# First-layer scores from exact high and low parts in one-pass products, keys one attention ahead, and a result whose heads stay in SBUF

## The chip, the core and the metric

The program runs on one core of a Trainium2 chip. The metric is device time in microseconds. The kernel before took 924.34 us (median of 3 runs, 924.27 to 926.34). Its profile comes from one more execution, which took 923.17 us; the span that the profile shows of it is 921.2 us.

The engines appear by short names: PE (TensorE, matrix products; PEld is its loading of weights), DVE (VectorE), ACT (ScalarE), POOL (GpSimd) and SP (SyncE, which here issues DMAs). SBUF is the memory on the chip that the engines compute from, PSUM the memory that products are written to, DRAM the large memory outside.

## The reference

16 sequences of 256 tokens with 256 features, and a context y of the same shape, go through three attentions of 16 heads (16 features a head) and one MLP:

```
layer 0: q = rms(x) Wq, k = rms(y) Wk, v = rms(y) Wv          (cross-attention, no positions)
         x = rms(x + softmax(q k^T / 4) v Wo)
layer 1: h = ln(x);  q, k, v from h; rotary positions on q, k;  causal;  x = x + a Wo
layer 2: h = ln(x);  q from h, k, v from y; rotary positions;   not causal;  x = x + a Wo
MLP:     x = x + gelu(ln(x) W1 + b1) W2                        (256 -> 1024 -> 256)
```

All of it is float32. The attention of a head is a product of 256 x 16 queries with 16 x 256 keys (the *scores*), an exponential, and a product of the result with the values; sums of the exponentials come from an extra column of the values, and the division is done on the result.

## The kernel before

**Attentions in one list.** The 48 attentions (3 layers x 16 sequences) stand in one hand-written order, `ORDER`, in which each digit is a layer: `000001010102210210210121021012210101021212122222`. Attention `i` is the i-th digit. The loop over `i` (with `n` for its blocks) writes out the order on every engine by hand: while attention `i` computes scores and values, the pieces for `i + 1` (query, key, value products), the end of `i - 1` and `i - 2` (heads, reciprocal, division, output product) and the statistics of `i + 2` are put between its blocks. Each engine runs its instructions strictly in that order; semaphores hold one back until its inputs are there. SP's queue of DMAs is in order too, so a DMA that waits holds up those behind it.

**Blocks.** An attention that isn't causal has 4 blocks: two tiles `t` of 8 heads, times two halves `kc` of the 256 keys. A causal one (layer 1) has 3. In block `n`, TensorE does the scores of block `n` (`scores`, line 569), then the values of the block before (`value`, line 609), then one dense product of 256 x 256 x 256 (`by_feature`, line 352, or `by_token`, line 364): the query, key or value of the next attention, or the output product of the last but one. In a causal attention the middle block has two dense products.

**Scores.** A tile of 128 partitions has 8 heads of 16 features, in four groups of 32 partitions with 2 heads each. A product contracts over a group of 32 and so over both heads. The query is therefore kept twice in `qm` (index `i` of 2), each copy with the other head's 16 partitions set to zero by a multiplication with `parity`. One product takes 64 keys and 2 x 256 queries (one column range for each copy); eight of them, on 4 row groups and 2 column groups of the array, make a block. ScalarE then takes the exponential of the four PSUM banks, in two instructions of 128 x 1024 (line 581). The tag `S` has two buffers, and a block uses both, so its scores wait for the exponentials of the block before.

**First layer's query and key.** `q` (line 487) writes both masked copies with two VectorE instructions from PSUM, times `rq`, the reciprocal norms of x spread over the partitions; `rq` is sent to DRAM and read back on all partitions (`send`, `receive`). `k` copies the key out of PSUM on ScalarE (line 527).

**The result's way.** The values' product leaves 32 partitions for each head (16 features, a sum, unused ones). `take` copies them to `av_sb` (line 626) and writes that to DRAM (line 627); `end` reads the sums (line 634) and the 16 features of each head (line 639) back, into a dense `oT`. `invert` takes reciprocals of the sums, sends them through DRAM to get them on all features of a head (lines 648, 654), and `divide` multiplies (line 660).

**The MLP** runs after the attentions on pairs of sequences, with 7 products for 8. Sums of its weights for that (`combine`, line 725) are made on GpSimd between the attentions.

Of the kernel before, what the change touches and what calls it, by code (L numbers as in the profile page):

```python
# [8 lines left out]
F32 = mybir.dt.float32  # L9
U8 = mybir.dt.uint8  # L10
I32 = mybir.dt.int32
AF = mybir.ActivationFunctionType
ALU = mybir.AluOpType
AX = mybir.AxisListType

P = 128
# [12 lines left out]
N_ATT = 3 * B  # L29

# [13 lines left out]
SWAP = [(i // HD) * HD + (i + HD // 2) % HD for i in range(32)]  # L44
# [29 lines left out]
def xattn_kernel(  # L74
# [45 lines left out]
    def batch(b):  # L120
# [3 lines left out]
        ys[b] = work.tile([P, NC, D], F32, tag="y", name=f"y{b}", bufs=3)  # L124
# [125 lines left out]
    def mean_squares(src, tag):  # L250
        ms = small.tile([P, NC], F32, tag=f"ms_{tag}", name=f"ms_{tag}")
        for c in range(NC):
            sq = work.tile([P, D], F32, tag="sq", name="sq", bufs=1)
            nc.vector.scalar_tensor_tensor(  # L254
                sq, src[:, c, :], 1.0 / D, src[:, c, :], ALU.mult, ALU.mult,
                accum_out=ms[:, c : c + 1],
            )
        return ms
# [112 lines left out]

    class Att:
        def __init__(self, i):
# [16 lines left out]
            self.pts = {}  # L390

# [17 lines left out]
        def spread(self):  # L409

            self.rq = work.tile([P, S], F32, tag="rq", name="rq")
# [21 lines left out]
        def receive(self):  # L433
            if self.layer == 0 and self.i > 1:
                self.rq = work.tile([P, S], F32, tag="rq", name="rq")
# [44 lines left out]

        def q(self, both=True):
            ps = by_feature(self.hT, self.w, 0)
            self.qm = work.tile([P, KC, 2, S], F32, tag="qm", name="qm", bufs=2)
# [14 lines left out]
        def second_mask(self):  # L498
            if self.layer > 0:
                nc.scalar.activation(  # L500
                    self.qm[:, :, 1, :], self.rotated_q, AF.Copy, scale=parity[1]
                )

        def first_qk(self):


            self.qm = work.tile([P, KC, 2, S], F32, tag="qm", name="qm", bufs=2)
            self.kT = work.tile([P, KC, S], F32, tag="kT", name="kT", bufs=2)
# [11 lines left out]
        def k(self):  # L520
            ps = by_feature(self.kvT, self.w, D)
            self.kT = work.tile([P, KC, S], F32, tag="kT", name="kT", bufs=2)
# [6 lines left out]
        def v(self):  # L529
            ps = by_token(self.kvT, self.w, 2 * D)  # L530
            va = self.va
            if self.layer == 0:
                m2 = slice(NC * self.b, NC * self.b + NC)
                nc.gpsimd.tensor_copy(
                    va[:, :, :, 16], mask01[:, m2].unsqueeze(2).to_broadcast([P, NC, H])
                )
                for c in range(NC):
                    nc.vector.tensor_scalar(
                        va[:, c, :, 0:HD], ps[:, c, :].rearrange("p (h d) -> p h d", d=HD),
# [3 lines left out]
            else:  # L543
                row = R_SAV if self.layer == 1 else R_CAV
                nc.gpsimd.memset(va[:, :, :, 16], 1.0)
                nc.vector.tensor_tensor(
                    va[:, :, :, 0:HD], ps.rearrange("p c (h d) -> p c h d", d=HD),
# [5 lines left out]
        def scores(self, n):  # L553
# [7 lines left out]
            pss = [psS.tile([P, 2, 512], F32, tag="S", name="S") for g in range(2)]  # L561
            for u, (t, _) in enumerate(units):
                for half in range(2):
                    keys = slice(64 * half, 64 * half + 64)
                    at = slice(kc * P + 64 * half, kc * P + 64 * half + 64)
                    for g, ps in enumerate(pss):
                        for j in range(2):
                            r = slice(32 * (2 * g + j), 32 * (2 * g + j) + 32)
                            nc.tensor.matmul(  # L569
                                ps[keys, j, 2 * m * u : 2 * m * (u + 1)]  # L570
                                .rearrange("p (i s) -> p i s", i=2),
                                lhsT=self.kT[r, t, at],
                                rhs=self.qm[r, t, :, q0:S],
                                start=True, stop=True, skip_group_check=True,
                            )
# [23 lines left out]
        def value(self, t, kc):  # L599
# [15 lines left out]
            if final and t == 0:  # L615
                self.av_sb = work.tile([P, KC, 2, S], F32, tag="av", name="av")
                self.sums = work.tile([P, 2, 2 * H], F32, tag="sums", name="sums")
                self.oT = work.tile([P, KC, S], F32, tag="oT", name="oT")

                self.hop = dram.tile([KC, 2, P, S], F32, tag="hop", name="hop")  # L620
                self.take(t, nc.scalar.copy)

        def take(self, t, copy):

            av = self.av_sb[:, t]
            copy(av, self.av)  # L626
            nc.sync.dma_start(out=self.hop[t].rearrange("i p q -> p i q"), in_=av)

        def end(self, copy=nc.vector.tensor_copy):


            self.take(1, copy)
            heads = self.hop.rearrange("t i (r e) q -> (t i r) e q", e=32)
            nc.sync.dma_start(
                out=self.sums[:, 0],
                in_=heads[:, HD, :].rearrange("g (a b) -> g a b", b=2 * H),
            )
            for t in range(KC):
                nc.sync.dma_start(out=self.oT[:, t], in_=heads[8 * t : 8 * t + 8, :HD])

        def invert(self, beside=lambda: None):

            sums = self.sums
            if self.layer == 0:
                nc.vector.tensor_scalar(sums[:, 0], sums[:, 0], 1e-30, None, ALU.max)
            nc.vector.reciprocal(sums[:, 1], sums[:, 0])
            hop = dram.tile([KC, 8, S], F32, tag="inv", name="inv_hop")
            nc.sync.dma_start(
                out=hop.rearrange("t g (a b) -> (t g a) b", b=2 * H), in_=sums[:, 1]
# [3 lines left out]
            for t in range(KC):  # L653
                nc.sync.dma_start(
                    out=self.inv[:, t], in_=hop[t].unsqueeze(1).to_broadcast([8, HD, S])
# [46 lines left out]
    up_s = [ctile([P, H1], f"up_s{n}") for n in (1, 2, 4)]  # L702
    down_t = [ctile([P, FF // P // 2, H2], f"down_t{n}") for n in (1, 2, 4)]
# [7 lines left out]
    def combine():  # L711

        s1, s2, s4 = up_s
        t1, t2, t4 = down_t
        for o, a, b, op in (
            (s1, up_a(1, 0), up_a(1, 1), ALU.add),
            (s2, s1, up_a(0, 0), ALU.subtract),
            (up_a(1, 0), up_a(0, 0), up_a(1, 0), ALU.subtract),
            (s4, up_a(0, 1), s2, ALU.subtract),
# [6 lines left out]
            yield  # L726

    class Mlp:
# [106 lines left out]
        def up(self, n):  # L835
# [6 lines left out]
            elif n == 5:  # L842
                self.Z = psS.tile([P, 2, 512], F32, tag="S", name="upZ")
                self.Z = [self.Z[:, i] for i in range(2)]
                self.up_product(5, self.Z, up_s[0], ts[0], True)
                self.keep_sum(1, 1, self.Z)
            elif n == 6:
                self.up_product(6, self.X, up_s[1], ts[1], False)
# [8 lines left out]
            elif n == 3:  # L857
                self.up_product(3, self.Z, up_s[2], b(1, 1), False)
# [793 lines left out]
```

## Time and profile before

| | |
|---|---|
| time, median of 3 runs | 924.34 us |
| the profiled execution, its span | 923.17 us, 921.2 us |
| TensorE busy | 908.0 us (99%) |
| VectorE busy | 684.6 us (74%) |
| ScalarE busy | 531.7 us (58%) |
| GpSimd busy | 346.5 us (38%) |
| scores (line 569) | 197.8 us busy, 3072 records |
| values (line 609) | 188.8 us busy, 3072 records |
| granted clock of TensorE | full, in all slices |
| bytes moved by DMA | 100.72 MB, 109 GB/s |

The attentions take up the span to about 735 us, the MLP the rest. A float32 product of the program shows as two records on TensorE. Records of products that run side by side overlap, so the busy time of a row, not count times mean, is what it takes.

### The profile page before, as it was taken

The numbers are of one execution on the slowest core, as the hardware profiler recorded it, in microseconds if no ns is written. First come the engines' busy times: TensorE is split into PE (matmuls) and PEld (weight loads), VectorE is DVE, ScalarE is ACT, GpSimd is POOL, SyncE is SP. The second block draws the span as 40 slices with busy tenths as digits, with TensorE's granted clock in tenths as the row PEclk, the third lists the DMA queues.
The fourth block names the chain that finished last, engine by engine and source line by source line (L and its number), as shares of the span: only waits on it lengthen the run. The fifth ranks groups of instructions, "written<-read, shape, count | busy, mean of one in ns | idle before, by whom it ended". The sixth has DMA issues, their size and how long they took to land.

```text
span 921.2 us, 32418 instructions
## 1 busy us (share of the span) xinstructions
PE 908.0 (99%) x13762; PEld 520.5 (57%) x13762; DVE 684.6 (74%) x1501; ACT 531.7 (58%) x744; POOL 346.5 (38%) x558
## 2 busy tenths in 40 slices
PE   8999999999999999999999999999999999999997
PEld 4444444445444444444444444445444799999997
DVE  4458777896978787958977768887887597777663
ACT  3666655766666665756655666666666633344440
POOL 4224764436454474542554433354133031111100
PEclk9999999999999999999999999999999999999999
DMA  9433554445343343433444433333222111112201
GB/s 294 159 115 111 169 158 137 139 147 146 99 131 98 114 138 108 133 104 107 140 142 138 131 100 101 96 97 106 87 82 85 37 49 55 44 62 69 71 25 49
DMA packets 112205, 100.72 MB, mean 109 GB/s; under 512 B 24299, under 2 KB 104051, under 8 KB 112051
## 3 DMA queue, kind: packets, MB, share of 16 engines
q1 hardware_dynamic: 106962, 83.59, 28.9%
q0 software_dynamic: 4400, 14.42, 5.1%
q8 instruction: 110, 1.80, 0.8%
q10 hardware_dynamic: 688, 0.54, 0.2%
q14 instruction: 45, 0.36, 0.1%
HBM read 59.70 MB, written 38.82 MB: 107 GB/s over the span
## 4 chain that ended last, share of the span: by engine, by line
PE 87%; DVE 7%; DMA 3%; issue 1%; ACT 0%; SPq 0%; POOL 0%; ACTq 0%; DVEq 0%; POOLq 0%
PE S L569 18%; PE A L609 16%; PE d L352 15%; PE d L364 15%; PE upX L792 6%; PE A L890 5%; PE downZ L890 3%; PE upZ L792 3%; PE d L890 2%; PE d L792 2%; DVE a L476 1%; DVE u L476 1%; DVE u L472 1%; DMA inv_hop<-sums 1%; DVE a L492 1%
## 5 line engine op out<-in xcount | busy, mean ns | idle before, releaser
L581 ACT ACTIVATE pt<-S 128x1024 f32<-128x1024 f32 x224 | 217.4, 1023 | 131.5 <-PE S L569 131.4
L569 PE MATMUL S<-qm,kT 32*64 32x512 f32 (+1 forms) x3072 | 197.8, 575 | 4.8 <-DVE kT L525 4.5
L609 PE MATMUL A<-pt,va 128*32 128x256 f32 (+1 forms) x3072 | 188.8, 367 | 0.2
L609 PEld LDWEIGHTS A<-pt,va 128*32 128x32 f32 x3072 | 80.1, 109 | 163.0 <-issue 99.8
L581 ACT ACTIVATE pt<-S,sy 128x1024 f32<-128x1024 f32 x128 | 135.8, 1112 | 50.1 <-PE S L569 50.1
L588 POOL TENSOR_SCALAR_AFFINE_SELECT pt<-pt 128x512 f32<-128x512 f32 x128 | 86.6, 691 | 139.6 <-ACT pt L581 139.3
L569 PEld LDWEIGHTS S<-qm,kT 32*64 32x64 f32 x3072 | 47.4, 130 | 77.4 <-issue 41.0
L468 ACT ACTIVATE a<-d,qk_bias 128x256 f32<-128x256 f32 x128 | 53.8, 471 | 49.7 <-PE d L352 33.4
L340 POOL TENSOR_TENSOR cur<-cur,bias 128x512 f32<-128x512 f32 x48 | 68.2, 1427 | 31.5 <-DVE xn L271 31.3
L352 PE MATMUL d<-hT,sa 128*32 128x256 f32 x1024 | 61.2, 379 | 0.0
L246 POOL TENSOR_SCALAR r_ln<-bmv 128x2 f32<-128x2 f32 x48 | 12.8, 266 | 125.3 <-DVE bmv L265 123.9
L476 DVE TENSOR_TENSOR a<-a,turn 128x512 f32<-128x512 f32 x64 | 55.3, 864 | 2.2
L814 ACT COPY g<-upX 128x512 f32<-128x512 f32 x28 | 15.0, 590 | 72.3 <-issue 67.4
L660 DVE TENSOR_TENSOR oT<-oT,inv 128x512 f32<-128x512 f32 x48 | 39.9, 832 | 21.3 <-issue 9.3
L476 DVE TENSOR_TENSOR u<-u,turn 128x512 f32<-128x512 f32 x64 | 52.9, 826 | 0.0
L472 DVE STREAM_SHUFFLE u<-a 128x512 f32<-128x512 f32 x64 | 47.5, 742 | 0.0
L830 ACT ACTIVATE g<-g,fb 128x256 f32<-128x256 f32 x96 | 41.1, 501 | 11.1 <-DVE g L819 11.1
L352 PEld LDWEIGHTS d<-hT,sa 128*32 128x32 f32 x1024 | 33.7, 110 | 21.5
L626 DVE COPY av<-A 128x512 f32<-128x512 f32 x47 | 32.0, 680 | 18.6 <-PE A L609 17.9
L246 POOL TENSOR_SCALAR r_o<-ms_o 128x2 f32<-128x2 f32 x16 | 4.7, 295 | 104.5 <-DVE sq L254 97.4
L271 DVE TENSOR_SCALAR xn<-cur,bmv,r_ln 128x256 f32<-128x256 f32 x96 | 41.6, 483 | 0.8 <-POOL r_ln L247 0.8
L885 DVE TENSOR_TENSOR g<-g,g 128x512 f32<-128x512 f32 x64 | 40.6, 682 | 0.0
(158 smaller groups left out, 1589.3 us busy)
## 6 DMA issues: line engine op xcount, KB each, us to landing
hop<-av SPq DMA_DIRECT2D x96, 256.0 KB
oT<-hop SPq DMA_DIRECT2D x96, 128.0 KB
inv<-inv_hop SPq DMA_DIRECT2D x96, 128.0 KB
turn_hop<-turn SPq DMA_DIRECT2D x33, 256.0 KB
hT<-turn_hop SPq DMA_DIRECT2D x132, 64.0 KB
out<-res SPq DMA_DIRECT2D x15, 256.0 KB
cur<-in_x POOLq DMA_DIRECT2D x11, 256.0 KB, 3.8
y<-in_y POOLq DMA_DIRECT2D x11, 256.0 KB, 4.6
```

Of the source, the lines that this page charges most:

```text
L340: nc.gpsimd.tensor_tensor(t, t, bias_sb[:, row : row + D].unsqueeze(1).to_broadcast([P, NC, D]), ALU.add)
L352: nc.tensor.matmul(o, lhsT=w[:, k, at + t * P + j : at + t * P + j + 32], rhs=tokens, start=(k == 0), stop=(k == KC - 1), skip_group_check ...
L364: nc.tensor.matmul(ps[j : j + 32, c * D : (c + 1) * D], lhsT=some_tokens(src, k, c, j), rhs=w[:, k, at : at + D], start=(k == 0), stop=(k ...
L468: nc.scalar.activation(a[:, t], ps[:, t], AF.Identity, bias=bias[:, t : t + 1])
L472: nc.vector.stream_shuffle(u.rearrange("p t s -> p (t s)"), a.rearrange("p t s -> p (t s)"), SWAP)
L476: nc.vector.tensor_tensor(t, t, table.unsqueeze(1).to_broadcast([P, KC, S]), ALU.mult)
L569: nc.tensor.matmul(ps[keys, j, 2 * m * u : 2 * m * (u + 1)] .rearrange("p (i s) -> p i s", i=2), lhsT=self.kT[r, t, at], rhs=self.qm[r, t, ...
L581: nc.scalar.activation(pt[:, :, :w], ps[:, :, :w], AF.Exp, scale=scale)
L588: nc.gpsimd.affine_select(out=diag, in_=diag, compare_op=ALU.is_ge, fill=0.0, base=0, pattern=[[0, 2], [0, 2], [1, P]], channel_multiplier=-1,
L609: nc.tensor.matmul(self.av[32 * r : 32 * r + 32, i, q0:S], lhsT=self.va[:, kc, 8 * t + 2 * r + i, :], rhs=pts[r // 2][:, r % 2, i * m : (i ...
L792: nc.tensor.matmul(o if len(b.shape) == 2 else by_groups(o), lhsT=a[:, c * P : (c + 1) * P], rhs=b, start=(first and c % 2 == 0), stop=Tru ...
L890: nc.tensor.matmul(ps[:, c, :], lhsT=a[f // 2][:, f % 2, c * P : (c + 1) * P], rhs=b[:, f, :], start=(first and c == 0 and f == 0), stop=True,
```

## The change

1. **One-pass products.** For first-layer attentions from the third on (`fast(i)`: layer 0 and `i > 1`, 14 of 16), query and key are each split into a high part, rounded to the type float32r, and a low part, what remains, also written as float32r. The features of two neighbouring heads are interleaved (even partitions one head, odd ones the other), by reordering the weights' columns on the host. The key goes to a tile `kd` in which, for each head of a pair, high and low parts fill even and odd partitions; the query to a tile `qd` in which both hold the same value. A product over 32 partitions then gives (k_high + k_low) times one part of the query. A block has 16 products of 128 keys x 256 queries: 2 heads of a pair x 2 parts of the query (added up in PSUM) x 4 row groups.
2. **New steps.** `q_high` (ScalarE), `q_low` (two on VectorE) and `q_out` (two DMAs from SBUF to SBUF, 256 KB each) for the query; `k_mm`, `k_high` (ScalarE), `k_low` (VectorE) and `k_out` (two DMAs) for the key.
3. **Keys an attention ahead.** The key of a fast attention `i + 2` is multiplied during attention `i`, and sent when `i`'s last scores are issued. Where `i` is not causal and `i + 1` isn't fast (`shifted`, 11 attentions), this takes the first block's dense product; query, key and value of `i + 1` move one block later.
4. **Heads from SBUF to SBUF.** `take` writes no DRAM; `sums_in` reads the sums (two DMAs) and `heads_in` the heads (four) straight from `av_sb`. During an attention before a fast one, `heads_in` comes after the reciprocal's DMAs, and `divide` one attention later, in the second block.
5. **Room and order.** Fewer buffers for `y` and `rq`, no own tile for `sq`; the MLP's weight sums use tiles of the attentions, and are made from attention 37 on. Some early loads are issued a few blocks later, and the loads of a later sequence in another order.

```diff
+F32R = mybir.dt.float32r
+FAST = (0,)
-SWAP = [(i // HD) * HD + (i + HD // 2) % HD for i in range(32)]
+SWAP = [(i + HD) % 32 for i in range(32)]
...
+    def fast(i):
+        return 1 < i < N_ATT and ORDER[i] in FAST
...
+        def query_tile(self):
+            return work.tile([P, 2, 2, KC, S], F32, tag="qm", name="qm", bufs=2)
+        def key_tile(self):
+            return work.tile([P, 2, KC, S], F32, tag="kT", name="kT", bufs=2)
...
         def q(self, both=True):
             ps = by_feature(self.hT, self.w, 0)
-            self.qm = work.tile([P, KC, 2, S], F32, tag="qm", name="qm", bufs=2)
+            if self.fast:
+                self.qd = self.query_tile()
+                self.qa = work.tile([P, KC, S], F32, tag="a", name="qa")
+                rq = self.rq.unsqueeze(1).to_broadcast([P, KC, S])
+                nc.vector.tensor_tensor(self.qa, ps, rq, ALU.mult)
+                return
+            self.masked_tile()
...
+        def q_high(self):
+            nc.scalar.copy(
+                self.qd[:, :, 0].rearrange("p i t s -> p i (t s)").bitcast(F32R),
+                self.qa.rearrange("p t s -> p (t s)").unsqueeze(1).to_broadcast([P, 2, KC * S]),
+            )
+        def q_low(self):
+            nc.vector.tensor_tensor(
+                self.qd[:, 0, 1].bitcast(F32R), self.qa, self.qd[:, 0, 0], ALU.subtract
+            )
+            nc.vector.tensor_copy(self.qd[:, 1, 1].bitcast(F32R), self.qd[:, 0, 1])
+        def q_out(self):
+            for i in range(2):
+                rows = self.qd[:, i].rearrange("p h t s -> p (h t s)")
+                nc.sync.dma_start(out=rows[1 - i : P : 2], in_=rows[i:P:2])
+        def k_high(self):
+            self.hl = work.tile([P, 2, KC, S], F32, tag="hl", name="hl", bufs=1)
+            nc.scalar.copy(self.hl[:, 0].bitcast(F32R), self.ps_k)
+        def k_low(self):
+            nc.vector.tensor_tensor(
+                self.hl[:, 1].bitcast(F32R), self.ps_k, self.hl[:, 0], ALU.subtract
+            )
+        def k_out(self):
+            self.kd = self.key_tile()
+            for i in range(2):
+                nc.sync.dma_start(
+                    out=self.kd[:, i].rearrange("p t s -> p (t s)"),
+                    in_=self.hl[i:P:2].rearrange("p h t s -> p h (t s)"),
+                )
...
+                for i in range(2):
+                    at = m * (2 * u + i)
+                    for h in range(2):
+                        for r, ps in rows:
+                            nc.tensor.matmul(
+                                ps[:, at : at + m],
+                                lhsT=self.kd[r, i, t, kc * P : (kc + 1) * P].bitcast(F32R),
+                                rhs=self.qd[r, i, h, t, q0:S].bitcast(F32R),
+                                start=(h == 0), stop=(h == 1), skip_group_check=True,
                             )
...
         def take(self, t, copy):
-            av = self.av_sb[:, t]
+            av = self.av_sb[:, :, t]
             copy(av, self.av)
-            nc.sync.dma_start(out=self.hop[t].rearrange("i p q -> p i q"), in_=av)
+        def heads_in(self):
+            for t in range(KC):
+                for i in range(2):
+                    nc.sync.dma_start(
+                        out=self.oT[64 * i : 64 * i + 64, t], in_=self.av_sb[0:P:2, i, t]
+                    )
+        def sums_in(self):
+            for i in range(2):
+                nc.sync.dma_start(
+                    out=self.sums[64 * i : 64 * i + 64, 0],
+                    in_=self.av_sb[1:P:32, i].rearrange("p t (a b) -> p (t a) b", b=2 * H),
+                )
...
+            shifted = i > 0 and fast(i + 2) and not a.causal and not fast(i + 1)
             for n in range(len(a.blocks)):
...
                 a.scores(n)
+                if n == len(a.blocks) - 1 and i > 0 and fast(i + 2):
+                    do(i + 2, "k_out")
...
-                    do(i - 1, "end")
-                    do(turns.get(i - 1), "pieces_in")
+                    do(i - 1, "take_last")
+                    if fast(i + 1):
+                        do(i + 1, "q")
+                    hasty = fast(i + 1)
+                    do(i - 1, "sums_in")
+                    if not hasty:
+                        do(i - 1, "heads_in")
+                        do(turns.get(i - 1), "pieces_in")
...
-                    if i + 1 < N_ATT:
+                    if shifted:
+                        do(i + 2, "k_mm", "k_high", "k_low")
+                    elif i + 1 < N_ATT and not fast(i + 1):
                         att(i + 1).q(both=not a.causal)
+                    if fast(i + 1) and a.causal:
+                        do(i + 1, "q_high")
                 elif n == 1:
...
+                    if was_hasty:
+                        do(i - 2, "divide")
+                    if fast(i + 1):
+                        if not a.causal:
+                            do(i + 1, "q_high")
+                        do(i + 1, "q_low", "q_out")
+                    elif a.causal:
                         do(i + 1, "k", "second_mask")
+                    if hasty:
+                        do(i + 2, "send")
+                        last.invert(lambda: do(turns.get(i - 1), "pieces_in"))
+                        do(i + 2, "receive")
...
+                    if hasty:
+                        do(i - 1, "heads_in")
...
+                    if shifted:
+                        do(i + 1, "q")
...
                 if n == final - 1:
-                    do(i + 1, "v")
+                    if shifted:
+                        do(i + 1, "k")
+                    else:
+                        do(i + 1, "v")
...
                 if n == final:
+                    if shifted:
+                        do(i + 1, "v")
```

## The prediction

> **What bounds the kernel now.** I read the page first. Busy time by engine says that TensorE hardly ever stops:
>
> ```profile
> PE 908.0 (99%) x13762; PEld 520.5 (57%) x13762; DVE 684.6 (74%) x1501; ACT 531.7 (58%) x744; POOL 346.5 (38%) x558
> ...
> PE 87%; DVE 7%; DMA 3%; issue 1%; ACT 0%; SPq 0%; POOL 0%; ACTq 0%; DVEq 0%; POOLq 0%
> ```
>
> The second line is the chain that ended last: 87% TensorE. A busy TensorE need not be at its peak, so next the windows (us of each engine in a stretch) over the attentions, and the waits for the idle time that TensorE does have:
>
> ```profile
> core 0: us, PE busy (x) PEld busy (x) DVE busy (x) ACT busy (x) POOL busy (x), PEclk, DMA share, GB/s
> 200.00:600.00 400.00, 397.60 (x7108) 190.35 (x7104) 315.53 (x672) 254.24 (x320) 188.41 (x294) 1.00 0.39 120
> ```
>
> ```profile
> PE S L569 <- DVE kT L525: 4.5, 5, 1.3
> ```
>
> So in 400 us TensorE misses 2.4, at full clock. What its products take is the time, until something takes its place; VectorE at 79% is next, and its late key tile is the one wait that reaches TensorE. How long a block's stages take I read from start to start in the timeline of attention 8 (first layer):
>
> ```profile
> 135.49 1.11 PE L569 MATMUL S<-qm,kT 32*64 32x512 f32 x16
> 136.53 1.07 PE L609 MATMUL A<-pt,va 128*32 128x256 f32 x16
> 136.76 2.12 ACT L581 ACTIVATE pt<-S,sy 128x1024 f32<-128x1024 f32 x2 [0.29 <-PE S L569]
> 137.42 1.91 PE L352 MATMUL d<-hT,sa 128*32 128x256 f32 x32
> 139.26 1.11 PE L569 MATMUL S<-qm,kT 32*64 32x512 f32 x16
> ```
>
> Scores 1.04, values 0.89, one dense product 1.84: 3.77 us a block. ScalarE needs 2.12 of it.
>
> **Part 1: the one-pass scores.** They are used in 14 of the 16 first-layer attentions (all but 0 and 1), 4 blocks each: 56 blocks. Before, a block has 8 products of 32x512, each recorded as two; eight tiles run at once. The values are 8 products on 4 tiles, so 2 rounds of 256 columns: 0.445 us a round (a dense product, 4 rounds, 0.46). At 0.445 the 512 columns of the scores are 0.89, which leaves 0.15 for starting in another tile shape. After, 16 products of 256 columns run on 4 tiles, 4 rounds. These numbers are for type float32, which the skill's page "FP8 and Floating Point Precision" ("TensorE Precision Notes") says takes 4 passes. If one pass is a quarter, a round streams in 0.111: 0.445 in all.
>
> No row shows a one-pass product of this type, so the cost is bounded. Weights decide: each round loads 128 columns per tile for only 0.111 us of streaming. The nearest row is the last layer's down product, which also loads 128 columns for a short stream (128 columns at half of the four passes, 0.111 by the same rate):
>
> ```profile
> L890 PE MATMUL A<-fc,g 128*128 128x128 f32 x224 | 27.3, 275 | 0.0
> L890 PEld LDWEIGHTS A<-fc,g 128*128 128x128 f32 x224 | 26.7, 192 | 0.4
> ```
>
> 27.3/224 = 0.122 us per load and product, so there the load hides behind the stream. Whether four row groups load side by side shows in the loads of the old scores:
>
> ```profile
> 195.25 0.23 PEld L569 LDWEIGHTS S<-qm,kT 32*64 32x64 f32 x16 [0.41 <-issue]
> 210.34 0.66 PEld L569 LDWEIGHTS S<-qm,kT 32*64 32x64 f32 x32 [0.41 <-issue]
> ```
>
> Sixteen loads of 130 ns end within 0.23: they overlap. My value: 4 x 0.122 + 0.15 = 0.64, a saving of 0.40 a block, 22.4 us in all. Lower end 0.445 + 0.15 = 0.60 (saving 25). Upper end, all 16 loads one after another, 16 x 0.119 + 0.15 = 2.05 (57 us lost).
>
> A rule speaks against the change. The Trainium skill, "TensorE: Matmul & The Clock Gate", section "The mechanism", lets a load overlap running products only if it is for another row group or goes to the background buffer; its section "LDWEIGHTS (loading the stationary operand)" prices a load by columns, P/1.2, so 107 ns for 128, whatever the rows. If the loads of one row group did not hide, a round would be 0.111 + 0.107 and the block 4 x 0.218 + 0.15 = 1.02: next to nothing gained. The row of the down product has loads for the same rows, and takes 0.122 instead of 0.218, so I go by the row. The same page's "Measured speedup vs the span model" has four row tiles reach 3.07 times rather than 4: by that the stream is 16 x 0.111/3.07 = 0.58, the block 0.73 and the saving 17 us. The loads in the trace overlap nearly fully (16 x 130 ns in 0.23 us), so I stay with 0.64.
>
> **Part 2: what the high and low parts cost elsewhere.** VectorE, per attention: the two masked writes go (2 x 742 ns). In come the scaled query (like 689, PSUM in), the low query (692 for two SBUF operands, 1058 where that is slow), its copy (480 to 680) and the low key (689): 2.55 to 3.12 us, net +1.1 to 1.6, 15 to 23 us over 14. VectorE has 84 of 400 us free; hidden unless it is late in order. ScalarE gains one copy of 128x1024, about 1.1 (as its exponential of that size, 1.112), to lie between exponentials: a block leaves 3.77 - 0.40 - 2.12 = 1.25. Hidden; uncovered it would cost 14 x 1.1 = 15.
>
> One block loses cover. With keys made an attention ahead, attention 3's second block has no dense product (the order of the built program shows it as the only one). There ScalarE sets the pace: scores to exponential 1.27 - 0.40 = 0.87, plus 2.12, is 2.99 against 0.64 + 0.89 = 1.53 on TensorE: +1.5.
>
> **Part 3: the new wait.** A query now crosses SBUF by DMA before its first score. Eleven of the 14 follow a causal attention, the shortest cover. Timeline of causal attention 7, which starts at 118.65:
>
> ```profile
> 118.65 1.12 PE L569 MATMUL S<-qm,kT 32*64 32x512 f32 x16 [1.00 <-DVE kT L525]
> 122.02 0.65 DVE L626 COPY av<-A 128x512 f32<-128x512 f32 x1
> 122.59 1.22 DVE L674 SCALAR_TENSOR_TENSOR cur<-s,r_o,bias 128x256 f32<-128x256 f32 x2
> 122.70 0.37 SPq L627 DMA_DIRECT2D hop<-av  x1
> 123.74 0.68 DVE L660 TENSOR_TENSOR oT<-oT,inv 128x512 f32<-128x512 f32 x1
> 125.01 0.55 SPq L634 DMA_DIRECT2D sums<-hop  x1
> 127.95 0.22 DVE L645 TENSOR_SCALAR sums<-sums 128x32 f32<-128x32 f32 x1 [2.21 <-DMA sums<-hop]
> 131.28 1.11 PE L569 MATMUL S<-qm,kT 32*64 32x512 f32 x16
> ```
>
> Attention 7 lasts 12.63; with its key product moved out (1.84) 10.8 is the deadline. Counted from its start: the av copy ends at 4.0, scaled query 4.7; finish and division follow (1.15 + 0.6) to 6.4; the high part on ScalarE is done by 5.8; low part 7.0 to 7.4, copy 7.5 to 8.1; two issues of 0.37. A 256 KB write was usable 2.3 us after issue (122.70 to 125.01), so the second lands at 10.2 to 10.8; by the 2.9 of the sums' read (125.01 to 127.95) at 10.8 to 11.4. No row has SBUF to SBUF. Behind the query's wait on SP stand the reciprocal's hop, the turned pieces, the scale row and the heads; the division that waits for the heads moves to the next attention's second block, so 3 to 4 us of delay there is covered. I take 0.4 late, 11 times: +4.5. Ends 0 and 23 (2.1 late, if the landing takes 4.4).
>
> Keys for layer 1 or 2 move one block later in the 11 shifted attentions, where two dense products now end the attention. The VectorE chain of query and key took 8.3 us in one case (196.4, shuffle of the query, to 204.7, end of the key's add), and starts at a query ready at 7.8 (two blocks and a product's copy); in the five that are first-layer themselves, with blocks of 3.37, the deadline is 4 x 3.37 + 1.84 = 15.3, the key ready at 7.8 + 8.3 = 16.1, or 14.8 without the slow add of that case (2.03 for 0.69); in the other six, blocks of 3.77, it is 16.9. Zero taken, since 4.5 of such waits are in the time before already; if all came 1 late, 11.
>
> **Part 4: heads without DRAM.** Per attention 2 writes of 256 KB, 2 reads of 128 and one of 16 become 4 copies of 64 and 2 of 8. Issue time stays (2 x 0.38 + 0.55 + 2 x 0.58 = 2.5 us before; six at about 0.38 after). The sums arrive about 2 us sooner, which takes VectorE out of waits (16.2 + 14.5 us in the trace); not TensorE's time, but it pays for part 2. Early loads that move, and the eight 1.5 to 1.75 us weight sums on GpSimd that move to attentions 37 on, where GpSimd is 30% busy: 0, within 1 either way.
>
> **Sum.** 22.4 - 1.5 - 4.5 = 16.4, from the profiled run's 923.17 (its span is 921.2; the 2 us around it stay): 906.8. The median shown, 924.34, is 1.2 above that run, so 908.
>
> **Rivals.**
> 1. VectorE or ScalarE becomes the bound in part (for: 79% already, contended rows of 1058 against 692; against: sums come sooner). Key 1 us late in 11 attentions: 908 + 11 = 919, less what overlaps with the 4.5: I set 916.
> 2. The query DMA decides; slower side. Place: first scores of a fast attention after a causal one. It cancels the other gain of 20.9 once each of 11 is 1.9 late, that is, lands over 4 us after issue; at 2.4 late they lose 26.4: 930. For: one sums read took that long (issued 153.12, used 157.54). Against: a 4 KB row per partition, and the 2.3 above.
> 3. Weight loads don't hide: 924 - 1 + 6 = 929; one after another: 924 + 57 + 6 = 987. Against: the two load rows.
> 4. It isn't one pass: 16 x 0.445/4 + 0.15 = 1.93 a block, +50: with the 6, 980. Against: the name alone.
>
> **Chances.** Forecast 0.57 (900 to 914), rival 1 0.17 (914 to 921), no change 0.05, rival 2 0.13, rivals 3 and 4 0.08. About 0.3% (2.8 us) is what a measurement tells from no change. Faster 0.74, same 0.05, slower 0.21. Range 898 to 929: below, a block of 0.60 and no lateness (924.3 - 25 + 1.5 = 901) and most of the 4.5 of late keys back; above, most of rival 2.
>
> **What would show it.** Score groups of 16 one-pass records, start to values' start 0.64 +- 0.07: part 1. At 1.02 or more, rival 3. Waits of TensorE's scores on a query DMA: under 5 us in all for the forecast, 20 or more for rival 2. Keys late from VectorE, over 10 us in all: rival 1. VectorE's busy time up by 15 to 23, the DRAM hop gone from the DMA list, TensorE idle below 25.

## The result and the profile after

The changed kernel took 907.6 us (median of 4 runs, 906.94 to 909.28), the kernel before, run beside it, 924.5: ratio 0.9822, 95% interval 0.9808 to 0.9836: 16.5 us less by the ratio, 16.9 by the medians. The profiled execution took 907.57 us, its span is 905.9 (921.2 before).

From its page, the busy times, the chain that ended last, and the score groups of both kinds (line 648 one-pass, line 637 the old form, busy time, mean ns, idle time before):

```profile
PE 889.2 (98%) x13762; PEld 538.4 (59%) x13762; DVE 689.5 (76%) x1529; ACT 541.4 (60%) x758; POOL 339.4 (37%) x558
...
PE 84%; DVE 7%; DMA 4%; SPq 2%; issue 1%; ACT 1%; POOL 0%; ACTq 0%; DVEq 0%
...
L637 PE MATMUL S<-qm,kT 32*64 32x512 f32 (+1 forms) x2176 | 134.5, 559 | 4.0 <-DVE kT L591 3.3
...
L648 PEld LDWEIGHTS S<-qm,kT 32*128 32x128 f32 x896 | 30.9, 183 | 25.8 <-ACT pt L659 18.6
L648 PE MATMUL S<-qm,kT 32*128 32x256 f32 x896 | 43.2, 303 | 2.3 <-ACT pt L659 1.7
```

TensorE is still the bound. The scores went from 197.8 us busy to 134.5 + 43.2 = 177.7, 20.1 less. The weight loads of line 648 are busy for 30.9 us of those 43.2 and lie beside the products. TensorE's idle time grew from 13.2 to 16.7 us, and the chain has more DMA and SP in it. The windows over the same 400 us as before:

```profile
core 0: us, PE busy (x) PEld busy (x) DVE busy (x) ACT busy (x) POOL busy (x), PEclk, DMA share, GB/s
200.00:600.00 400.00, 395.79 (x7288) 204.39 (x7284) 321.21 (x706) 265.59 (x337) 185.53 (x303) 1.00 0.33 105
```

TensorE misses 4.2 us there instead of 2.4, at full clock; VectorE is at 80%. The same block of attention 8 as before, in the timeline (start, us, engine, line):

```profile
129.57 0.74 PE L648 MATMUL S<-qm,kT 32*128 32x256 f32 x16
...
130.25 1.07 PE L687 MATMUL A<-pt,va 128*32 128x256 f32 x16
130.43 2.12 ACT L659 ACTIVATE pt<-S,sy 128x1024 f32<-128x1024 f32 x2
...
131.13 1.91 PE L354 MATMUL d<-hT,sa 128*32 128x256 f32 x32
...
132.97 0.75 PE L648 MATMUL S<-qm,kT 32*128 32x256 f32 x16
```

From start to start: scores 0.675 (before 1.04), values 0.89, dense product 1.84: 3.40 us for 3.77. That is 0.37 a block, 56 x 0.37 = 20.7 us. What TensorE waits for, by the waits (us in total, times, longest):

```profile
PE S L637 <- DVE kT L591: 3.3, 6, 0.8
PE idle L1096 <- POOL zeros L191: 2.1, 1, 2.1
PE d L354 <- DMA hT<-turn_hop: 2.1, 1, 2.1
PE S L648 <- ACT pt L659: 1.7, 4, 0.6
...
PE S L648 <- DMA qm<-qm: 0.5, 1, 0.5
```

I then laid every block of attentions 2 to 46 beside the time that its own TensorE work takes. What is over was 9.3 us before (without 0.9 us of extra products in attention 11) and is 16.3 after: 7.0 more. Attentions 0 and 1 went the other way. In the old kernel the last block of attention 0 had no dense product (2.41 us) and the next one waited for exponentials (4.77). The key product of attention 2, 1.84 us of work, moved into that hole; now the two take 3.77 each, so only 0.36 of it is paid. Small differences included, 1.6 us are gained up to attention 2. The account: -20.7 - 1.6 + 7.0 = -15.3, which is 921.2 - 905.9.

### The profile page after: what moved, and what is told of

Its sections match the earlier page's. It is cut to its first block, busy times and chain, and to the rows that moved or that the text cites. A ratio compares the mean times of both kernels' runs of the same rounds, so it can differ in the third digit from the quotient of the medians.

```text
span 905.9 us, 32810 instructions
## 1 busy us (share of the span) xinstructions
PE 889.2 (98%) x13762; PEld 538.4 (59%) x13762; DVE 689.5 (76%) x1529; ACT 541.4 (60%) x758; POOL 339.4 (37%) x558
## 4 chain that ended last, share of the span: by engine, by line
PE 84%; DVE 7%; DMA 4%; SPq 2%; issue 1%; ACT 1%; POOL 0%; ACTq 0%; DVEq 0%
PE A L687 16%; PE d L354 16%; PE d L366 14%; PE S L637 13%; PE upX L908 6%; PE A L1006 6%; PE downZ L1006 3%; PE upZ L908 3%; PE S L648 3%; PE d L1006 2%; PE d L908 2%; DMA sums<-av 1%; DVE a L483 1%; DVE u L483 1%; DVE u L479 1%
## 5 line engine op out<-in xcount | busy, mean ns | idle before, releaser
L637 PE MATMUL S<-qm,kT 32*64 32x512 f32 (+1 forms) x2176 | 134.5, 559 | 4.0 <-DVE kT L591 3.3
L637 PEld LDWEIGHTS S<-qm,kT 32*64 32x64 f32 x2176 | 34.4, 130 | 53.1 <-issue 31.9
L483 DVE TENSOR_TENSOR a<-a,turn 128x512 f32<-128x512 f32 x64 | 52.5, 820 | 2.2
L648 PEld LDWEIGHTS S<-qm,kT 32*128 32x128 f32 x896 | 30.9, 183 | 25.8 <-ACT pt L659 18.6
L648 PE MATMUL S<-qm,kT 32*128 32x256 f32 x896 | 43.2, 303 | 2.3 <-ACT pt L659 1.7
L749 DVE TENSOR_TENSOR oT<-oT,inv 128x512 f32<-128x512 f32 x48 | 36.6, 762 | 7.4 <-DMA oT<-av 5.2
```

The source lines that it names most:

```text
L483: nc.vector.tensor_tensor(t, t, table.unsqueeze(1).to_broadcast([P, KC, S]), ALU.mult)
L637: nc.tensor.matmul(ps[64 * half : 64 * half + 64, 2 * m * u : 2 * m * (u + 1)] .rearrange("p (i s) -> p i s", i=2), lhsT=self.kT[r, t, at] ...
L648: nc.tensor.matmul(ps[:, at : at + m], lhsT=self.kd[r, i, t, kc * P : (kc + 1) * P].bitcast(F32R), rhs=self.qd[r, i, h, t, q0:S].bitcast(F ...
```

## The experiments

Each kernel is the changed one with the edit shown. Where single waits are compared, it is by blocks of the profiled executions.

**1. The products off.**

```diff
-FAST = (0,)
+FAST = ()
...
-                    if i == 0:
+                    if i == 0 and fast(2):
                         do(2, "k_mm", "k_high", "k_low", "k_out")
```

> After, but no attention uses the one-pass products: scores, masked queries and keys are those of before; heads from SBUF to SBUF, moved loads and moved weight sums stay. My theory: the products bring 20.7 us (56 blocks, 3.77 to 3.40) and bring with them about 7 us of new waits; the rest of the change brings about 1.6 at the start and costs about 1.9 by the weight sums. So this kernel should stand at 922 to 925. Rival: the result's shorter way is worth several us of its own, and this kernel is at 919 or lower. Second rival: the products bring more than the whole gain and the rest costs; then it is over 927.

It took 923.93 us, ratio to before 0.9993 (0.9984 to 1.0003): no change. So the products, with the key order that they need, bring the gain of some 16 us, and the rest of the change is worth nothing in sum. By blocks that zero is two parts: up to attention 36 this kernel is 2.2 us ahead of the one before (attentions 6, 22, 29 and 30 no longer end late), and from 37 to 43, where the weight sums are now made, it loses 3.4. The gain in attentions 0 and 1 isn't in it (2.41 and 4.77 as before), so that one belongs to the moved key product.

**2. Half the rounds.** The products with the low part of the query are left out.

```diff
-                    for h in range(2):
+                    for h in range(1):
...
-                                start=(h == 0), stop=(h == 1), skip_group_check=True,
+                                start=(h == 0), stop=(h == 0), skip_group_check=True,
```

> After, but the products with the low part of the query are left out: 8 products of 128x256 in a block instead of 16, 2 rounds for 4. If a round costs 0.122 (a load of 128 columns) and the rest of 0.675 us is the start in another tile shape, a block's scores take 0.43 and 56 blocks bring 13 to 14 us: 893 to 895, unless ScalarE (2.12 us of exponential in a block that would last 3.15) ends more waits. Rival: most of 0.675 is fixed, a round costs 0.05 or less: 902 or more.

**3. The same columns, twice the loads.**

```diff
-                        for r, ps in rows:
+                        for c, (r, ps) in ((c, row) for c in (0, m // 2) for row in rows):
                             nc.tensor.matmul(
-                                ps[:, at : at + m],
+                                ps[:, at + c : at + c + m // 2],
...
-                                rhs=self.qd[r, i, h, t, q0:S].bitcast(F32R),
+                                rhs=self.qd[r, i, h, t, q0 + c : q0 + c + m // 2].bitcast(F32R),
```

> After, but each product of 256 queries is made as two of 128 with the same keys: as many columns stream, twice as many loads of 128 columns. If the load sets the pace (0.122 a round), 8 rounds take 0.98 and a block's scores 1.13 for 0.675: 56 x 0.46 = 25 us slower, 930 to 935. If the stream sets the pace (0.111 for 256 columns), the loads hide and nothing changes: 907 to 910. In between: loads of a row group hide only behind part of the stream.

A round is four products side by side, one on each row group. One block of each kernel in the timeline, first with half the rounds, then with twice the loads; the scores last from the first line's start to the second's:

```profile
140.18 0.51 PE L648 MATMUL S<-qm,kT 32*128 32x256 f32 x8
...
140.62 1.07 PE L687 MATMUL A<-pt,va 128*32 128x256 f32 x16
```

```profile
133.84 1.11 PE L648 MATMUL S<-qm,kT 32*128 32x128 f32 x32
...
134.88 1.07 PE L687 MATMUL A<-pt,va 128*32 128x256 f32 x16
```

Two rounds take 0.44 us, four 0.675: (0.675 - 0.44) / 2 = 0.1175 a round, and 0.675 - 4 x 0.1175 = 0.205 that doesn't depend on the rounds. Eight rounds of half the columns take 1.04. Taking the same 0.205 off would leave 0.104 a round, but it is not the same there: the first round takes 0.164 us with half the columns and 0.223 with all (medians, from one round's first product to the next one's). So the middle rounds are read directly: they start 0.112 us apart with 128 columns and 0.118 with 256. Half the columns save next to nothing, so it is not the stream that sets the 0.112; nor is it the issue of the products, as the four of a round start within 13 ns of each other (in 95 of 100 rounds). What is left is the load of 128 columns, at about 0.112, with four row groups loading side by side; a stream of 256 columns hides it almost fully. If load and stream added up, four rounds would take about twice as long. The two are about equal: the tile shape gives no further gain from shorter streams.

The times did not follow the blocks. Twice the loads: 923.9 us (0.9987, 0.997 to 1.0003), against the 930 to 935 expected with a load-paced block of 1.13; its scores cost 56 x 0.365 = 20.4 more than after, and 5.4 of waits went. Half the rounds: 905.37 us (0.9788, 0.9771 to 0.9805), against 893 to 895, although the block did what was expected. By blocks, 12.5 us were lost in attentions 2 to 10 (up to 2.5 of them, in attention 2, in another execution of the changed kernel too, see 9). The greater part are waits; TensorE's idle time is 24.0 us for 16.7:

```profile
PE S L637 <- DVE kT L591: 7.5, 6, 3.0
PE S L648 <- ACT pt L659: 3.2, 4, 1.7
PE S L648 <- DMA qm<-qm: 2.8, 2, 2.0
```

VectorE's key is up to 3.0 us late, and the query's DMA 2.0. In these early attentions, where first-layer ones stand close together, VectorE's chains and the DMAs are the next bound, right behind TensorE.

About 5 us are no waits but TensorE's clock. The windows of one such place, with the same columns as above (PEclk is the third number from the end):

```profile
117.06:120.47 3.41, 0.45 (x14) 0.07 (x8) 3.34 (x8) 0.00 (x0) 0.00 (x0) 1.00 0.71 248
120.47:123.88 3.41, 3.41 (x32) 1.08 (x36) 3.30 (x10) 1.33 (x2) 1.28 (x3) 0.50 0.05 17
```

In the first stretch TensorE waits nearly throughout, for VectorE's key; in the second it is busy throughout, but at half the clock, and loses 1.7 us. The same stands at 55.6 and 76.1 us, behind stretches in which TensorE was busy for 1.07 and 1.42 of 3.41 us. The profile of the changed kernel has no such place before its last 2 us. It is not this one execution alone: the four runs with half the rounds have mean clocks of 0.994 to 0.997, the nine of the changed kernel 0.997 to 1.0. So a long wait can cost more than its length.

**4. The query sent twice.**

```diff
-                nc.sync.dma_start(out=rows[1 - i : P : 2], in_=rows[i:P:2])
+                for _ in range(2):
+                    nc.sync.dma_start(out=rows[1 - i : P : 2], in_=rows[i:P:2])
```

> After, but each of the two query copies from SBUF to SBUF is made twice, the second one waiting for the first: the query is complete some 2.5 to 3 us later, and what stands behind it on SP's queue too. The prediction had the query 0.4 late in 11 attentions: then all 11 pay the whole delay, 28 to 33 us, 935 to 940. My reading of the trace now: about 1 to 1.5 us of slack, so 11 to 20 us, 918 to 928. Rival: 3 us or more of slack, 907 to 911.

It took 1002.87 us (1.083, 1.079 to 1.087): worse than any expectation, because the delay was larger than I had set it, and because the clock fell as well. SP and TensorE at attentions 7 and 8, from the timelines of short stretches:

```profile
145.53 0.52 SPq L545 DMA_DIRECT2D qm<-qm  x1
...
147.85 1.15 SPq L545 DMA_DIRECT2D qm<-qm  x2
...
152.57 0.47 SPq L545 DMA_DIRECT2D qm<-qm  x1
...
155.27 0.80 PE L649 MATMUL S<-qm,kT 32*128 32x256 f32 x8 [2.57 <-DMA qm<-qm]
```

The first copy, alone on the queue, lands 2.3 us after issue; the second is then issued together with a third, and the fourth, which waits for the third, goes out only 4.7 us later. The query is complete 9.7 us after the first issue. In the changed kernel the two copies go out at 121.75, the scores start at 125.54 and their second half at 125.88, neither with a wait, so both copies were there within 4.1 us:

```profile
121.75 1.16 SPq L544 DMA_DIRECT2D qm<-qm  x2
123.30 0.32 SPq L737 DMA_DIRECT2D inv_hop<-sums  x1
123.72 1.83 SPq L319 DMA_DIRECT2D hT<-turn_hop  x4
...
125.54 0.75 PE L648 MATMUL S<-qm,kT 32*128 32x256 f32 x16
```

From the start of attention 7 to the second half of 8's first scores it is 16.9 us instead of 11.3: 5.6 later. How late the query is, this run alone doesn't say, since in the changed kernel it may be there some time before it is used; experiment 5 uses the same query 3.4 us after issue without a wait, so it is at least 9.7 - 3.4 = 6.3 us later here. Most of the delay is paid, and the slack is 0.7 us or more. (My reading of 1 to 1.5 is not excluded.)

The delay is not all that was paid. TensorE was busy for 920.6 us instead of 889.2 with the same products, and idle for 64.4 us more; the page shows why it was busy longer, and the windows around 152.71, where it waits for attention 8's query, show how:

```profile
PEclk9997898899799999898998988999999999999999
```

```profile
149.30:152.71 3.41, 0.59 (x12) 0.33 (x8) 0.69 (x1) 0.33 (x1) 1.99 (x4) 1.00 0.95 332
152.71:159.54 6.83, 4.27 (x52) 2.61 (x56) 0.69 (x2) 2.12 (x2) 0.00 (x0) 0.50 0.50 164
```

In 13 stretches of 3.4 to 10.2 us, 85 us in all and the end of the program aside, the granted clock is 0.50, each time behind 3.41 us in which TensorE was busy for 0.51 to 1.44 us. It is busy for 60 us of the 85, of which half, 30 us, is lost: that accounts for the longer busy time. The same holds in attention 8: 1.9 us more are lost after 155.27, without any wait, in 4.27 us of work at half the clock. The first blocks of all 14 fast attentions, 3.9 to 6.7 us longer, have waits in them and, in all but attention 3's, the clock.

**5 and 6. The turned pieces.** In attention 13 of the changed kernel, SP issues the reads of the next turned tile behind the query's copies, and TensorE waits for them (timeline):

```profile
208.46 1.16 SPq L544 DMA_DIRECT2D qm<-qm  x2
209.71 0.54 SPq L737 DMA_DIRECT2D inv_hop<-sums  x1
210.35 3.12 SPq L319 DMA_DIRECT2D hT<-turn_hop  x4
...
216.50 1.93 PE L354 MATMUL d<-hT,ca 128*32 128x256 f32 x32 [2.07 <-DMA hT<-turn_hop]
```

Two remedies: the reads ahead of the query on SP (5), or on ScalarE's queue (6):

```diff
-                    if not hasty:
-                        do(i - 1, "heads_in")
-                        do(turns.get(i - 1), "pieces_in")
+                    if not hasty:
+                        do(i - 1, "heads_in")
+                    do(turns.get(i - 1), "pieces_in")
...
-                        last.invert(lambda: do(turns.get(i - 1), "pieces_in"))
+                        last.invert()
```

> After, but the four reads of the turned pieces are issued on SP before the query's two copies instead of behind them and the sums' reciprocal. The 2.1 us wait of attention 14's first block goes. But the double copy showed that the query has no slack: four issues take 1.8 us, and where the pieces' hop has not landed, SP waits for it with the query behind. Expected: 2 us gained once, 1 to 2 us lost in each of five to ten attentions: 910 to 920. Rival: the query has a microsecond or more of slack, and the kernel takes 905.5.

```diff
-                        last.invert(lambda: do(turns.get(i - 1), "pieces_in"))
+                        if turns.get(i - 1) is not None:
+                            att(turns[i - 1]).queue = nc.scalar
+                        do(turns.get(i - 1), "pieces_in")
+                        last.invert()
```

> After, but those reads of the turned pieces that stood behind the query's copies on SP are issued on ScalarE's queue, in the second block. Then neither holds up the other: attention 14's 2.1 us go, and nothing else is late, 905 to 906. Rival: four issues of some 0.5 us on ScalarE between two exponentials make the exponentials late, and it takes 908 or more.

In both, attention 14's first block went from 6.12 to 3.84 us. The first took 908.14 us (0.9813, 0.9791 to 0.9835), no gain in sum. Where the reads were moved, the query went out 0.2 to 1.15 us later relative to its attention. In attentions 6 and 8 it was 0.7 later and cost 0.04 or less; in 24 the scores waited 1.0 instead of 0.5; and in 36 the query went out 1.15 later, was used all the same without a wait, and the first block was 0.09 longer:

```profile
517.12 1.16 SPq L544 DMA_DIRECT2D qm<-qm  x2
...
519.76 0.83 PE L648 MATMUL S<-qm,kT 32*128 32x256 f32 x16
```

So there was a microsecond of slack in one place, 0.7 or more in two, none in another; my 910 was too pessimistic. The second took 906.33 us (0.9792, 0.977 to 0.9815), as expected; its interval overlaps that of the changed kernel, so the gain is shown by the block and not by the time.

**7. The weight sums later.**

```diff
-                if n in (1, 3) and combined and not a.causal:
+                if (n == 3 or i == 46 and n == 2) and combined and not a.causal:
```

> After, but the eight weight sums on GpSimd are not made in the second and fourth blocks of attentions 37 to 43, but in the last block of each non-causal attention from 37 to 46 (and one in the third block of 46), where VectorE has no key to bring in time. If a sum beside VectorE's key chain is what makes attentions 37 and 43 end late (VectorE's product of 0.69 us took 1.66 beside it), their waits of 0.8 and 0.7 go: 1.5 to 2 us, 905.5 to 906.5. Rival: the key chain there is late in any case since those keys come after a causal attention; then the waits stay.

906.53 us (0.98, 0.9776 to 0.9825), an interval that again overlaps that of the changed kernel. The last blocks of attentions 37 and 43 became 0.87 and 0.76 us shorter, and that of 45, which got a sum, 0.67 longer. What happens in 37, in the timeline of the changed kernel, and of this one:

```profile
547.16 1.43 POOL L814 TENSOR_TENSOR down_t<-fc,down_t 128x512 f32<-128x512 f32 x1
547.38 1.49 DVE L518 TENSOR_SCALAR qm<-a,vec 128x512 f32<-128x512 f32 x1
...
552.22 1.12 PE L637 MATMUL S<-qm,kT 32*64 32x512 f32 x16 [0.79 <-DVE kT L591]
```

```profile
546.19 0.47 DVE L518 TENSOR_SCALAR qm<-a,vec 128x512 f32<-128x512 f32 x1
```

The masked write of the query takes 1.49 us beside a sum and 0.47 without; the key comes behind it on VectorE, and TensorE waits 0.79 us for the key. The rival, a key late in any case, is out.

**8. Keys of the shifted attentions in the third block.**

```diff
                 if n == final - 1:
                     if shifted:
-                        do(i + 1, "k")
+                        do(i + 2, "k_mm", "k_high", "k_low")
```

(and q, k of `i + 1` in the first and second block, as without the shift)

> After, but in the 11 shifted attentions the key of i+2 is multiplied in the third block instead of the first, so query and key of i+1 stay in the first and second as before. My theory: the waits of 0.5 to 0.8 us at the start of attentions 5, 7, 9, 18 (scores that wait for VectorE's key) come from the key's move one block later, and go: 2.4 us, about 905. Rival: VectorE is late there for its own load, and the waits stay or move to the query of i+2.

910.59 us (0.9839, 0.9805 to 0.9874), no gain. The waits for VectorE's key at the start of 5, 7, 9 and 18 were gone, as the theory had it (0.71, 0.68, 0.54 and 0.74 off the blocks before; the last was missing in all later executions, so it is no evidence). But TensorE's timeline shows new ones:

```profile
102.04 1.93 PE L354 MATMUL d<-hT,sa 128*32 128x256 f32 x32 [1.16 <-DMA hT<-turn_hop]
...
130.70 1.93 PE L354 MATMUL d<-hT,sa 128*32 128x256 f32 x32 [1.56 <-DMA hT<-turn_hop]
```

The query of `i + 1` needs its turned pieces, which stand behind the query of `i` on SP. The shift that makes keys late covers these pieces.

**9. The corrections together,** beside the unaltered changed kernel on the same chip. "Three orders" has the moves of 6 and 7 (without attention 45's sum), and in attention 2 the key product one block later; there ScalarE had waited for the one buffer of the parts. "Four orders" adds that of 8.

```diff
+                    elif i == 2:
+                        do(i + 1, "v")
...
+                    if i == 2:
+                        do(i + 2, "k_mm", "k_high", "k_low")
...
+                if (n == 3 and i != 45 or i == 46 and n == 2) and combined and not a.causal:
```

> The changed kernel itself, unaltered, on the same chip as the two that follow, since what they should bring is below what differs between chips: 906 to 909.

> After, with three things moved: the turned pieces behind the query's copies on ScalarE's queue, the weight sums in last blocks (not that of attention 45), and in attention 2 the key product of attention 4 in the third block instead of the second, so that ScalarE doesn't wait there for the low and high parts' one buffer. Theory: 2.1 + 1.6 + 1 us, 902 to 904. Rival: what one wait gives back the next takes, 906 or more.

> The same, and in the 11 shifted attentions the key of i+2 in the third block. Alone that move cost time, because the query of i+1 then came before its turned pieces (TensorE waited 1.2 and 1.6 us for them in attentions 6 and 8), while the waits for VectorE's key at the start of 5, 7 and 9 were gone. With the pieces on ScalarE's queue they should be there in time, and the move bring its 2 us: 900 to 902. Rival: ScalarE's queue is not early enough for pieces needed one block sooner, and it is no faster than the kernel with three.

Unaltered 909.17 us (0.9824, 0.9801 to 0.9846), three orders 905.17 (0.9785, 0.9762 to 0.9808), four orders 905.43 (0.9786, 0.9768 to 0.9805). The three bring about 4 us, though the intervals just overlap; the fourth brings nothing. Each mended wait is gone in the profiles: attention 2 is 1.2 us shorter, 14 2.3, 37 0.87, 43 0.76. Yet attentions 3 to 5 lost 4.8 us in the profile with three and 4.0 in the one with four, where the timeline shows the query of attention 4:

```profile
66.33 1.15 SPq L544 DMA_DIRECT2D qm<-qm  x2
...
72.72 0.50 PE L648 MATMUL S<-qm,kT 32*128 32x256 f32 x8 [1.95 <-DMA qm<-qm]
```

Issued at 66.33, it was waited for until 72.7. Part of the losses is the clock again. It was at 0.50 for 3.41 us from 89.9 on with three orders (the first block of attention 5, 1.6 us longer) and from 73.8 on with four (the first block of attention 4, up to 1.7). The profile of the unaltered kernel taken beside them, too, has 2.5 us more in attention 2 than its first profile (4.59 and 5.99 for 3.63 and 4.40), and 1.6 of them are the same:

```profile
51.83:55.24 3.41, 1.67 (x30) 0.73 (x26) 0.67 (x3) 2.79 (x4) 0.65 (x3) 1.00 0.90 347
55.24:58.65 3.41, 3.41 (x38) 1.89 (x42) 1.31 (x3) 2.41 (x3) 0.00 (x0) 0.50 0.08 19
```

How much of the other 3.2 and 2.3 us in attentions 3 to 5 the moves cause, and how much differs from one execution to the next, stays open.

## Why the prediction was right, and where it wasn't

The time came out as forecast (908 against 907.6); of its terms, some did not.

- **Scores.** Predicted block 0.64, saving 22.4; measured 0.675, saving 20.7. The round was right (0.122 from the row of the down product, 0.1175 measured); the start in another tile shape was 0.205, not 0.15. The choice of the row over the rule held. The Trainium skill, "TensorE: Matmul & The Clock Gate", section "LDWEIGHTS (loading the stationary operand)", prices a load of 128 columns at 107 ns; experiment 3 comes near it with 0.112. But added to the stream, as the prediction read the rule for loads of the same row group, it would have made the block 1.02, and experiments 2 and 3 show it hidden. The 3.07-fold overlap of the same page's "Measured speedup vs the span model" (block 0.73) was too pessimistic here.
- **Attention 3's block without a dense product.** 1.5 predicted; 0.44 and 1.00 over in two blocks, 1.44.
- **The query's DMA.** This is the mis-sized term: 4.5 predicted (0.4 late in each of 11), and the wait list has 0.5 in one place (attention 24, which lost 0.76). The chain to the issue was shorter than I set it: issued 7.1 us after its attention's start, where I had the copy's end at 7.5 to 8.1, because VectorE's steps took their short times (688 and 440 ns in the groups) and the two finishing steps before them 0.86 us for 1.15. The landing (2.3 alone; two within 3.0 in attention 36 of experiment 5, within 3.4 in 8) was inside my bounds. The warning under it held: of a delay of some 6.3 us experiment 4 shows 5.6 paid. But the slack was a microsecond in one place and none in another, and rival 2's price would have been higher than I put it, since long waits cost clock too.
- **Costed at nothing, and not nothing.** Turned pieces behind the query on SP: 2.1 us in attention 14; I had named them in the queue, but given only the heads their cover. The key chain of the shifted attentions: 0.5 to 0.7 each in 4, 6 and 8 (zero taken, 11 as the other end). Weight sums: 0.87 and 0.76 (0, within 1). The parts' one buffer in attention 2: 1.0 us and its neighbours, not thought of.
- **Not foreseen.** The key product of attention 2 filled a hole at the start: about 1.5 gained.
- **VectorE.** Up 4.9 us, not 15 to 23. The new rows are as counted (34.9 in, 19.6 out, 15.3 net), but old ones shrank: the rotated sum from 33.9 to 29.5, the cosine product from 55.3 to 52.5, the division 39.9 to 36.6 (one of the masked writes grew, from 12.9 to 15.1).
- **Heads without DRAM.** VectorE's waits for sums fell from 16.2 + 14.5 to 5.0 + 1.6 us. Experiment 1 puts the worth of it and the other moves at 2.2 us, taken back by the weight sums.

Against the forecast's 16.4 the terms are: scores 1.7 short, query 3.7 better, start 1.5 better, the result's shorter way 2.2 better, and 2.1 + 1.9 + 1.6 + 1.2 = 6.8 of small waits that had been set at zero (turned pieces, keys, sums, buffer). That makes 16.4 - 1.7 + 3.7 + 1.5 + 2.2 - 6.8 = 15.3. It closes better than it should: smaller waits, as 0.74 us in attention 17 and 0.5 in 9, are not in it. The sum was right because terms missed on both sides balanced, which is luck; only the first of them was argued well. None of the rivals happened.

## What to carry to other kernels

When one engine fills 98% of the time, price its new work from the nearest row of the same load and stream, and expect the rest to be small waits: a queue that is in order, a buffer that is single, a neighbour that holds the engine up. Each thing moved ahead of something on such a queue is to be asked for what stands behind it, and its cover named: here the turned pieces, not the query itself, cost the most. Cutting the bound further pays only as far as the next chains are away: the last 13 us off the scores brought 2 to 3. And a wait of a few microseconds on the engine that fills the time is to be priced at more than its length where the profile shows the clock falling behind such waits.

## What the hardware showed that I had not expected

- One-pass products of 32 x 128 tiles on four row groups: a load of 128 columns takes about 0.112 us and hides behind 256 columns of stream (0.118 a round), even for the same row group.
- TensorE's granted clock was 0.50 in 19 stretches of 3.4 to 10.2 us, in five of the profiles (experiments 2, 4 and 9; the last 3 us of a span aside). Each came right behind 3.41 us in which TensorE had been busy for 1.67 us or less. Not every such pause brings it: the changed kernel's profile has 3.41 us with 1.34 busy (from 213.1 us, attention 14) and full clock behind it. What decides between them, no run here shows.
- A 256 KB copy from SBUF to SBUF landed in 2.3 us when alone in nine attentions of experiment 4, and in 2.5 to 4.2 in the other five. Of two issued together the complete query was there within 3.0 us in one place of experiment 5, and beside the early loads it was waited for until 6.4 us after issue. The landing differs with what else is under way.
- A masked write on VectorE took 1.49 us beside a GpSimd sum of 128 x 512, and 0.47 without; it ended 0.28 us after that sum.
